# Adding a turned partial result in PSUM: read in its order of storage, written through a view by columns

## The chip, the core and the metric

The kernel runs on one core of a Trainium2 chip. The metric is device time in microseconds (us) of one execution, the median over several runs. Lower is better.

## The reference

Two layers of a vision state-space model are applied in a row to x of 8 images, 64 by 64 positions, 192 channels. Each layer is `x = x + conv(gn(x))`: group normalisation, an input projection to 384 channels and a gate z, a depthwise 3 by 3 convolution with SiLU, a selective scan over the 4096 positions, layer normalisation over channels, multiplication with the activated gate, and an output projection.

The selective scan runs in several directions. In layer 0 there are two: by rows, forward and backward. In layer 1 there are four: by rows and by columns, each forward and backward. For each direction, every channel and each of 16 states:

```
h = exp(delta * A) * h + (delta * u) * B        # along the positions
y = sum over the 16 states of h * C
```

The y of all directions are summed at each position (a direction by columns has to be turned back to rows first), and the skip term `u * D` is added.

## The kernel before, in words

Each layer runs a `front` (normalisation, projections, convolution) and then `scans`. The change is in `scans`.

The positions of an image are cut into 8 chunks of T = 512, and the 384 channels into DT = 3 tiles of 128 partitions. A *step* i is one chunk of one direction of one image. Layer 0 has 8 x 2 x 8 = 128 steps, layer 1 has 8 x 4 x 8 = 256. Layer 1's directions are, in order: columns forward, columns backward, rows backward, rows forward. A step has NSL = 24 *slots*, one for each pair of states (8) and each channel tile (3). Within a slot:

- `inject` (L763, matmuls L773) lets TensorE write (delta * u) * B for two states into a PSUM tile `hb`. It runs two slots ahead, and `hb` has two buffers. Its moving operand takes two neighbouring floats out of every eight (L776).
- `decay` (L783, L790) lets ScalarE compute the factors `da`, four slots ahead.
- `scan` (L801) lets VectorE run two scans along the positions (L817), and after every third slot lets POOL multiply h by C (L820) into `hc`.
- `reduce` (L827) lets TensorE sum `hc` over the states into the PSUM tile `py` (3 banks of 512 floats).

`reduce` and `add_y` both use `block_diag` (L172, matmuls L176): four matmuls on 32 by 32 pieces of the array for each channel tile, so 12 for three tiles. TensorE's fp32 matmul shows as two records.

At the end of a step `keep_y` (L874) copies `py` to SBUF and `store_y` (L884) stores it to the DRAM tensor `yrow` or `ycol`. Before that, `add_y` (L868) adds into `py` what is already there to be summed: the input times the skip weights in the first direction, or an earlier direction's sum through `mask` (an identity in 32 by 32 pieces).

Layer 1's third direction is the first by rows after two by columns. It has to take the sum of the column directions, which lies in `ycol` by columns, and bring it into `py`, which lies by rows. `load_turned` (L851) issues DMAs in slots 8 to 19 which bring, for the chunk's RB = 8 image rows, 64 columns of 8 floats each into the tile `yt`: in SBUF the 8 floats of one image column lie together. The view `live[i]["y"]` (L856) reads this tile by rows, so that neighbouring elements of the view are 8 floats apart. `add_y` then runs in slot 27, which is three slots into the next step, and `keep_y` in slot 29.

The order of all instructions is written out by hand. `at(i, s, f, ...)` enters a function for slot s of step i, tables such as `L1_SLOTS` (L108) give the slots, and the loop at L1099 to L1111 issues `scan`, then the entries of the slot in order of rank, then `inject` for two slots later and `decay` for four slots later. The finishing work of the previous image (`f_...`: normalisation, gate, output projection) is entered in the same way.

The lines around the turned sum:

```
live[i]["yt"] = s1.tile([P, DT, T], F32, name="y")                            # L855
live[i]["y"] = live[i]["yt"].rearrange("p t (w h) -> p t h w", h=RB)          # L856
...
block_diag(nc, live[i]["py"], w, live[i]["y"][:, dt], dt, False, False)       # L872
...
at(i, slots["add_turned"], add_y, i)                                          # L1048
```

Of the kernel before, what the change touches and what calls it, by code (L numbers as in the profile page):

```python
# [18 lines left out]
W = 64  # L19
# [9 lines left out]
RB = T // W  # L29
# [18 lines left out]


L0_SLOTS = {  # L50
    "turn_b": 1,
    "keep_b": 2,
    "dt_proj": (6, 3, 4),
# [52 lines left out]
    "f_add": (111, 113),  # L106
}
L1_SLOTS = {  # L108
    "x_proj": (1, 1, 3),
    "x_dbl": 4,  # L110
    "turn_b": 7,
# [60 lines left out]
def block_diag(nc, out, w, x, dt, first, last):  # L172

    for i in range(NQ):
        j = (i + dt) % NQ
        nc.tensor.matmul(  # L176
            out[j * Q : (j + 1) * Q, dt],
            w[i * Q : (i + 1) * Q],
            x[i * Q : (i + 1) * Q],
            start=first,  # L180
            stop=last,
            tile_position=(i * Q, j * Q),
        )
# [372 lines left out]
def scans(tc, name, x_src, x_dst, xcd, xcd_col, xtd, xdd, zd, t, dirs, rank, row_b, gate, slots, last, ends, consts, dram):  # L556
# [5 lines left out]
    nc = tc.nc  # L562
# [8 lines left out]
    def tiles(a):  # L571
        return a.rearrange("(t p) l -> p t l", p=P)
# [17 lines left out]
    with tc.tile_pool(name=f"{name}_s1", bufs=1) as s1, tc.tile_pool(  # L590
# [7 lines left out]
        def at(i, s, f, *a):  # L598
            todo.setdefault(i * NSL + s, []).append((f, a))

        live = {}
# [249 lines left out]
        def load_turned(i, j):  # L851

            b, k, cols, rev, ci, c = steps[i]
            if j == 0:
                live[i]["yt"] = s1.tile([P, DT, T], F32, name="y")  # L855
                live[i]["y"] = live[i]["yt"].rearrange("p t (w h) -> p t h w", h=RB)  # L856
            dt, q = divmod(j, 4)
            cs = slice(q * W // 4, (q + 1) * W // 4)
            yt = live[i]["yt"].rearrange("p t (w h) -> p t w h", h=RB)[:, dt, cs]
            yd = tiles(ycol[b % 2])[:, dt].rearrange("p (w h) -> p w h", h=H)[  # L860
                :, cs, c * RB : (c + 1) * RB
            ]
            e = dt * Q
            nc.sync.dma_start(out=yt[: P - e], in_=yd[e:])
            if e:
                nc.sync.dma_start(out=yt[P - e :], in_=yd[:e])

        def add_y(i):  # L868
            k = steps[i][1]
            for dt in range(DT):  # L870
                w = t["skip"][:, dt] if k == 0 else mask
                block_diag(nc, live[i]["py"], w, live[i]["y"][:, dt], dt, False, False)  # L872

        def keep_y(i):  # L874
            b, k, cols, rev, ci, c = steps[i]
# [3 lines left out]
        def same(i):  # L879

            b, k, cols = steps[i][:3]
            return k > 0 and dirs[k - 1][0] == cols and b < B - 1
# [131 lines left out]
        def thrice(i, s, f, *a):  # L1014
            for p, q in enumerate(s):
                at(i, q, f, *a, p)

        for i in range(N):
            j = i - 1
            live[i] = {}  # L1020
            at(j, -3, load_xt, i)
            if xdd is None:
                at(j, -8, load_x, i)
                thrice(j, slots["x_proj"], x_proj, i)
                at(j, slots["x_dbl"], x_dbl, i)
            else:
                at(j, -4, load_xdbl, i)
            at(j, slots["turn_b"], turn_b, i)
            at(j, slots["keep_b"], keep_b, i)
            for dt in range(DT):  # L1030
                for f in dt_proj, dt_bias, turn_delta, make_dut:
                    at(j, slots[f.__name__][dt], f, i, dt)
            at(j, slots["softplus"], dt_softplus, i)
            at(j, slots["softplus"] + 1, first_decays, i)
            at(j, 14, enter, i, 0)
            at(j, NSL + 1, enter, i, 1)
            at(i, -12, load_b, i, 0)
            at(i, 0, load_b, i, 1)
            for m in range(NP):
                at(i, 3 * m - 6, load_c, i, m)  # L1040
                at(i, 3 * m + 3, carry, i, m)
                for n in range(2):
                    at(i, 3 * m + slots["reduce"][n], reduce, i, m, n)
            b, k, cols, rev, ci, c = steps[i]
            if k and dirs[k - 1][0] != cols:
                for j in range(4 * DT):
                    at(i, 8 + j, load_turned, i, j)
                at(i, slots["add_turned"], add_y, i)  # L1048
            elif not same(i):
                at(i, 6, load_y, i)  # L1050
                at(i, slots["add_y"], add_y, i)
            at(i, slots["keep_y"], keep_y, i)
            at(i, slots["keep_y"] + 1 * same(i), store_y, i)
# [30 lines left out]
        for c in range(NCH):  # L1084
# [4 lines left out]
            for r, fs in enumerate(  # L1089
                (  # L1090
                    (f_act,),
                    (dt_proj, turn_b, turn_delta, f_turn, f_back, f_out, x_proj),
                    (reduce, add_y),
                    (load_b, load_c, load_turned),
                )
            )
            for f in fs
        }
        with tc.manual_schedule(engines=ENGINES):  # L1099
            g = min(todo)  # L1100
            while todo:
                i, s = divmod(g, NSL)
# [11 lines left out]
def vss_layer(tc, name, x_src, x_dst, w, dirs, rank, row_b, gate, slots, last, ends, consts, dram):  # L1114

    with ExitStack() as ctx:
        xcd, xcd_col, xtd, xdd, zd, *dram = dram
        if any(cols for cols, rev in dirs):
            xdd = None
        else:  # L1120
            xcd_col = None
        t = load_weights(tc, ctx, name, w, len(dirs), rank, row_b + 2 * NS, consts[1])
        clear = dram[-1] if xcd_col is None else ()
        early = gate if gate == AF.Silu else None
        front(tc, name, x_src, xcd, xcd_col, xtd, xdd, zd, w["in_proj"], early, t, clear, consts)
        late = gate if early is None else None
        scans(tc, name, x_src, x_dst, xcd, xcd_col, xtd, xdd, zd, t, dirs, rank, row_b, late, slots, last, ends, consts, dram)
# [3 lines left out]
def two_vss_layers(ctx, tc, x, grp_d, w0, w1, out):  # L1131
# [27 lines left out]
    dram = (xcd, xcd_col, xtd, xdd, zd, yrow, ycol, cscr, dgd)  # L1159
    vss_layer(tc, "l0", x, mid, w0, L0_DIRS, 12, 32, AF.Gelu, L0_SLOTS, L0_LAST, L0_ENDS, consts, dram)  # L1160
    vss_layer(tc, "l1", mid, out, w1, L1_DIRS, 96, 96, AF.Silu, L1_SLOTS, L1_LAST, L1_ENDS, consts, dram)

# [63 lines left out]
```

## Time and profile before

| | us |
|---|---|
| median of 3 runs | 24904.81 (24903.24 to 24905.65) |
| profiled execution, its own time | 24896.44 |
| its span, first to last instruction | 24894.7 |
| start of layer 1's first and last scan | 9782.8 and 24837.6 |
| granted TensorE clock, mean | 0.994 of full speed |

| engine | what it does most | busy us |
|---|---|---|
| DVE (VectorE) | scans, L817 | 20778.5 |
| POOL (GpSimd) | h times C, L820 | 20742.4 |
| ACT (ScalarE) | decay factors, L790 | 12245.1 |
| PE (TensorE) | `inject`, L773 | 10887.2 |
| PE (TensorE) | `reduce`, L176 `py<-hc,mask` | 6870.0 |
| PE (TensorE) | `add_y` with the mask, L176 `py<-y,mask` | 204.0 |
| PE (TensorE) | `add_y` with the skip weights, L176 `py<-y,skip` | 156.5 |

How to read the lines: a group gives the line of the code, the engine, the operation, output<-input by the tiles' names, the shapes and the count, then busy time and the mean duration of one in ns, then the engine's idle time before them and what ended it. Busy time of TensorE counts the time in which at least one matmul ran; matmuls on different 32 by 32 pieces of the array run side by side, so the mean duration times the count is more than the busy time. PEld is the loading of weights, which overlaps matmuls.

### The profile page before, as it was taken

The page shows a single profiled execution, that of the slowest core. Times are in us where ns is not written, and L with a number is a line of the kernel's source. Part 1 is how long each engine was busy: PE and PEld are TensorE (multiplying, and loading weights), DVE is VectorE, ACT ScalarE, POOL GpSimd, SP SyncE. Part 2 cuts the span into 40 slices and gives each one's busy share as a digit, 9 for nine tenths or more (in the row PEclk, how much of TensorE's full clock was granted, in tenths as well). Part 3 has the DMA queues.
Part 4 walks back from the last instruction along what each step waited for, and adds up shares of the span by engine and source line. Part 5 has one row for each costly group of instructions (what it writes and reads, how often), then busy time and mean ns, then how long its engine had stood idle before and what let it go on. Part 6 is the DMA issues. An engine that isn't in the chain of part 4 may idle for free.

```text
span 24894.7 us, 773793 instructions
## 1 busy us (share of the span) xinstructions
PE 23122.6 (93%) x331456; PEld 13199.4 (53%) x331456; DVE 23113.1 (93%) x22416; ACT 19698.0 (79%) x39311; POOL 21490.1 (86%) x4439
## 2 busy tenths in 40 slices
PE   9989999999999898999999999999999999999998
PEld 3455555555555434555555555555555555555554
DVE  7799999999999877999999999999999999999997
ACT  6678888888888777777777877877877877877877
POOL 0299999999999802999999999999999999999998
PEclk9999999999999999999999999999999999999999
DMA  5566666667666556676676676676676676676675
GB/s 188 174 157 168 163 163 170 162 165 170 161 165 168 159 212 209 161 160 167 168 169 167 165 169 168 165 168 168 166 168 168 167 168 167 167 168 166 175 173 158
DMA packets 3857278, 4208.94 MB, mean 169 GB/s; under 512 B 2136204, under 2 KB 2368420, under 8 KB 3850788
## 3 DMA queue, kind: packets, MB, share of 16 engines
q1 hardware_dynamic: 3775472, 3970.30, 61.6%
q0 software_dynamic: 67200, 132.13, 3.1%
q8 instruction: 2626, 43.02, 0.7%
q10 hardware_dynamic: 11188, 57.00, 0.6%
q14 instruction: 792, 6.49, 0.1%
HBM read 3412.11 MB, written 746.65 MB: 167 GB/s over the span
## 4 chain that ended last, share of the span: by engine, by line
PE 23%; DVE 22%; ACT 8%; issue 5%; POOL 2%; DMA 0%; DVEq 0%; SPq 0%; POOLq 0%; ACTq 0%
DVE h L817 21%; PE hb L773 10%; PE py L176 8%; ACT da L790 4%; PE pd L613 3%; POOL hc L820 2%; PE pt L661 1%; ACT y L877 1%; PE po L997 1%; DVE dut L736 1%; ACT delta L169 1%; ACT da L798 1%; ACT L169 0%; ACT L685 0%; ACT xn_sq L957 0%
## 5 line engine op out<-in xcount | busy, mean ns | idle before, releaser
L820 POOL TENSOR_TENSOR hc<-h,cr 128x3072 f32<-128x3072 f32 x3072 | 20742.4, 6813 | 3292.9 <-DVE h L817 2088.6
L817 DVE TENSOR_TENSOR_SCAN h<-da,hb 128x512 f32<-128x512 f32 x18432 | 20778.5, 1198 | 1122.3 <-PE hb L773 940.6
L790 ACT ACTIVATE da<-delta,a_neg 128x512 f32<-128x512 f32 x18432 | 12245.1, 713 | 1303.1 <-DVE h L817 1286.4
L773 PEld LDWEIGHTS hb<-dg,dut 64*128 64x128 f32 x147456 | 9226.7, 185 | 6945.3 <-issue 5972.6
L773 PE MATMUL hb<-dg,dut 64*128 64x128 f32 x147456 | 10887.2, 286 | 897.4 <-DVE h L817 885.6
L176 PE MATMUL py<-hc,mask 32*32 32x512 f32 x147456 | 6870.0, 601 | 8.3 <-POOL hc L820 7.4
L176 PEld LDWEIGHTS py<-hc,mask 32*32 32x32 f32 x147456 | 1268.5, 103 | 1661.7 <-issue 1173.1
L798 ACT COPY da<-a 128x2 f32<-128x2 f32 x8064 | 1563.0, 194 | 287.5 <-ACT da L790 0.7
L398 DVE SCALAR_TENSOR_TENSOR tp<-pad,cw,tp 128x512 f32<-128x512 f32 x2112 | 1414.7, 746 | 188.9 <-ACT tp L392 168.1
L661 PE MATMUL pt<-xdbl,w_dt 96*128 96x512 f32 (+1 forms) x2304 | 1300.5, 646 | 36.7 <-ACT delta L675 22.7
L825 ACT COPY st<-h 128x6 f32<-128x6 f32 x2688 | 536.8, 200 | 999.7 <-DVE h L817 999.5
L728 PE MATMUL pq<-ident,delta 128*128 128x128 f32 x4608 | 758.8, 287 | 432.3 <-DVE dut L736 298.6
L877 ACT COPY y<-py 128x1536 f32<-128x1536 f32 x384 | 552.7, 1439 | 695.4 <-PE py L176 662.3
L675 ACT ACTIVATE delta<-pt,dtb 128x512 f32<-128x512 f32 x1152 | 790.8, 686 | 353.8 <-PE pt L661 353.4
L736 DVE TENSOR_TENSOR dut<-pq,xt_k 128x512 f32<-128x512 f32 x1152 | 767.4, 666 | 81.0 <-PE pq L728 81.0
L728 PEld LDWEIGHTS pq<-ident,delta 128*128 128x128 f32 x4608 | 484.5, 141 | 637.0 <-DVE dut L736 415.5
L613 PE MATMUL pd<-x_k,w_x 128*128 128x512 f32 x1536 | 797.3, 628 | 8.5 <-ACT xv L437 8.5
L346 PE MATMUL pi<-x,w_x 128*128 128x512 f32 x1536 | 756.1, 614 | 44.4 <-ACT xv L437 22.2
L997 PE MATMUL po<-yc,w_out 128*64 128x256 f32 (+1 forms) x2304 | 586.5, 468 | 13.4 <-ACT delta L675 8.3
L169 ACT ACTIVATE delta<-delta 128x1536 f32<-128x1536 f32 x384 | 570.5, 1486 | 4.3
L987 POOL TENSOR_TENSOR yc<-yc,g 128x512 f32<-128x512 f32 x384 | 497.9, 1314 | 20.7 <-ACT yc L978 16.3
L685 ACT ACT_TABLE_LOAD x384 | 492.7, 1283 | 6.8
(98 smaller groups left out, 9722.0 us busy)
## 6 DMA issues: line engine op xcount, KB each, us to landing
cr<-cscr SPq DMA_DIRECT2D x2048, 512.0 KB, 4.2
dg<-dgd SPq DMA_DIRECT2D x1536, 512.0 KB, 7.8
cr<-xdd SPq DMA_DIRECT2D x1024, 512.0 KB, 6.2
xt_k<-xtd SPq DMA_DIRECT2D x768, 384.0 KB, 7.1
yrow<-y SPq DMA_DIRECT2D x144, 768.0 KB, 6.7
zd<-zo SPq DMA_DIRECT2D x192, 512.0 KB, 3.0
xcd<-xo SPq DMA_DIRECT2D x128, 768.0 KB, 3.5
xtd<-xv SPq DMA_DIRECT2D x128, 768.0 KB, 3.6
```

Of the source, the lines that this page charges most:

```text
L176: nc.tensor.matmul(out[j * Q : (j + 1) * Q, dt], w[i * Q : (i + 1) * Q], x[i * Q : (i + 1) * Q], start=first, stop=last, tile_position=(i ...
L398: nc.vector.scalar_tensor_tensor(tv, window(dt, c, s), cw[:, dt, s : s + 1], tv, ALU.mult, ALU.add)
L613: nc.tensor.matmul(live[i]["pd"][:R], w_x[:, dt, k, :], live[i]["x"][:, dt], start=(dt == 0), stop=(dt == DT - 1),)
L661: nc.tensor.matmul(pt, w_dt[:, k, dt * P : (dt + 1) * P], live[i]["xdbl"][:rank], start=True, stop=True,)
L728: nc.tensor.transpose(pq[:, g], live[i]["delta"][:, dt, g * P : (g + 1) * P], ident)
L736: nc.vector.tensor_mul(live[i]["dut"][:, dt], live[i]["pq", dt], live[i]["xt"][:, :, dt * P : (dt + 1) * P])
L773: nc.tensor.matmul(hv[:, r, q], live[i]["dut"][r * G : (r + 1) * G, dt, q], dg[r * G : (r + 1) * G, q, :, 2 * mm : 2 * mm + 2], start=True ...
L790: nc.scalar.activation(da[:, n].rearrange("p (r g j) -> p r g j", r=2, j=G), live[i]["delta"][:, dt].rearrange("p (g r j) -> p r g j", r=2 ...
L798: nc.scalar.copy(da[:, :, f], live[i]["a0"][:, dt, 2 * m : 2 * m + 2])
L817: nc.vector.tensor_tensor_scan(o, a, v, init, ALU.mult, ALU.add)
L820: nc.gpsimd.tensor_mul(hc, h, cr)
L997: nc.tensor.matmul(o, w_out[:, dt, P:] if u else w_out[:, dt, :P], y, start=(dt == 0), stop=(dt == DT - 1), tile_position=(0, h * G),)
```

## The change

For the turned y, `add_y` reads the tile `yt` in the order in which it lies (64 columns of 8 floats, 512 in a row), and gives the matmul an output view of `py` in the same order: for each image column the 8 rows, which are 64 floats apart in PSUM. The same sums land in the same places. In the other uses of `add_y` nothing changes. The slots of `enter` and `load_b` are now read from the tables, with the values that stood in the code (the old `at(i, -12, ...)` is `at(j, 12, ...)` of the step before, j = i - 1).

```diff
 L0_SLOTS = {
+    "enter": 14,
+    "load_b": 12,
...
 L1_SLOTS = {
+    "enter": 14,
+    "load_b": 12,
...
                 live[i]["yt"] = s1.tile([P, DT, T], F32, name="y")
-                live[i]["y"] = live[i]["yt"].rearrange("p t (w h) -> p t h w", h=RB)
...
         def add_y(i):
             k = steps[i][1]
+            py, y = live[i]["py"], live[i].get("y")
+            if y is None:
+                y = live[i]["yt"].rearrange("p t (w h) -> p t w h", h=RB)
+                py = py.rearrange("p t (h w) -> p t w h", w=W)
             for dt in range(DT):
                 w = t["skip"][:, dt] if k == 0 else mask
-                block_diag(nc, live[i]["py"], w, live[i]["y"][:, dt], dt, False, False)
+                block_diag(nc, py, w, y[:, dt], dt, False, False)
...
-            at(j, 14, enter, i, 0)
+            at(j, slots["enter"], enter, i, 0)
...
-            at(i, -12, load_b, i, 0)
+            at(j, slots["load_b"], load_b, i, 0)
```

## The prediction, made before the changed kernel ran

> **What bounds the kernel now.** I read the page first. Four engines are busy for most of the span, so the shares name no bound.
>
> ```profile
> PE 23122.6 (93%) x331456; PEld 13199.4 (53%) x331456; DVE 23113.1 (93%) x22416; ACT 19698.0 (79%) x39311; POOL 21490.1 (86%) x4439
> ```
>
> Next I took the groups of instructions that write or read the tile py, because the change touches only those. Columns: engine, operation, count, then shortest, median and longest duration in ns.
>
> ```profile
> L176 PE MATMUL py<-y,skip x3072: 587/587/612, 1141.2 to 23341.1; 32*32 32x512 f32 x192
> L176 PE MATMUL py<-y,mask x2112: 587/1074/1097, 8176.1 to 24818.2; 32*32 32x512 f32 x192
> ```
>
> Each fp32 matmul leaves two records. Both rows have the same shape (32 by 32 weights, 512 columns), yet one has a median of 587 ns and the other of 1074. The count explains the second row. One `add_y` is 12 matmuls, so 24 records. `py<-y,mask` has 2112 = 88 x 24: 24 calls on a y loaded as it is used, all in the last image, and 64 calls (8 images by 8 chunks of layer 1's third direction) on the turned y. Counted one by one in the trace, all 64 turned calls have medians near 1084 and the others 587 to 600. The turned call reads single floats 8 floats apart (L856). A step of 32 B by itself is not what costs:
>
> ```profile
> L773 PE MATMUL hb<-dg,dut 64*128 64x128 f32 x147456 | 10887.2, 286 | 897.4 <-DVE h L817 885.6
> ...
> L728 PE MATMUL pq<-ident,delta 128*128 128x128 f32 x4608 | 758.8, 287 | 432.3 <-DVE dut L736 298.6
> ```
>
> `inject` (L773) reads pairs of floats, pair after pair 8 floats apart, and takes 286 ns for 128 columns, as much as the transposes of L728 (287), which read 128 floats in a row. So reading singles 32 B apart nearly doubles a record, reading pairs 32 B apart costs nothing. [...]
>
> Is the long call on the path? I compared TensorE's timeline, then VectorE's, at the place where the turned call runs (four slots into the next chunk's scan), once in layer 1's second direction, which adds no y there, and once in the third. Columns: start and length in us, instructions, idle time before them.
>
> ```profile
> 10301.77 2.12 PE L773 MATMUL hb<-dg,dut 64*128 64x128 f32 x32
> 10303.82 1.12 PE L613 MATMUL pd<-x_k,w_x 128*128 128x512 f32 x2
> 10304.87 1.11 PE L176 MATMUL py<-hc,mask 32*32 32x512 f32 x24
> 10305.92 1.19 PE L773 MATMUL hb<-dg,dut 64*128 64x128 f32 x16
> ```
>
> ```profile
> 10757.91 2.12 PE L773 MATMUL hb<-dg,dut 64*128 64x128 f32 x32
> 10759.96 1.12 PE L613 MATMUL pd<-x_k,w_x 128*128 128x512 f32 x2
> 10761.02 1.11 PE L176 MATMUL py<-hc,mask 32*32 32x512 f32 x24
> 10761.90 2.77 PE L176 MATMUL py<-y,mask 32*32 32x512 f32 x24
> 10764.60 1.19 PE L773 MATMUL hb<-dg,dut 64*128 64x128 f32 x16
> ```
>
> ```profile
> 10759.25 4.55 DVE L817 TENSOR_TENSOR_SCAN h<-da,hb 128x512 f32<-128x512 f32 x4 [1.12 <-PE hb L773]
> 10765.91 4.55 DVE L817 TENSOR_TENSOR_SCAN h<-da,hb 128x512 f32<-128x512 f32 x4 [2.10 <-PE hb L773]
> ```
>
> TensorE has no gap here. The next `inject` begins 4.15 us after the previous one without the turned call (10301.77 to 10305.92) and 6.69 us after it with the call. VectorE then waits 2.10 us for that `inject`; at the same place of the second direction (10303 to 10313) it scans without such a wait. Last, the table of busy time by stretches, over eight chunk bodies without a turned call and the eight of the same image with it (image 0), and the same for image 1:
>
> ```profile
> 10295.20:10751.40 456.20, 418.01 (x6368) 245.99 (x6368) 443.87 (x410) 354.49 (x701) 443.15 (x87) 1.00 0.63 153
> 10751.40:11225.60 474.20, 438.58 (x6560) 252.72 (x6560) 445.44 (x409) 354.42 (x701) 433.09 (x79) 1.00 0.77 165
> 12157.10:12624.50 467.40, 436.17 (x6456) 255.07 (x6453) 447.20 (x414) 371.95 (x754) 451.21 (x95) 1.00 0.65 160
> 12624.50:13105.10 480.60, 453.64 (x6646) 260.30 (x6644) 448.37 (x413) 371.80 (x753) 440.76 (x87) 1.00 0.79 172
> ```
>
> The first number is the length. In image 0 a turned call costs (474.20 - 456.20) / 8 = 2.25 us of time, all of the VectorE wait, and nothing gives it back within the chunk. From image 1 on the previous image's finishing work runs alongside, and the cost is (480.60 - 467.40) / 8 = 1.65 us on average: some of it lies beside other delays. So TensorE sets the time at these 64 places.
>
> **The change, part by part.** (1) The view of y in `load_turned` (L856) goes, and `add_y` now reads y in the order in which it lies. (2) The same 12 matmuls write PSUM through a view by columns: eight floats of one column of the image, each 64 floats from the last. (3) `enter` and `load_b` take their slots from the tables, with the same slots 14 and 12; the second counts 12 past the chunk before instead of 12 ahead of its own, which with 24 slots to a chunk is the same place. The instruction lists of both kernels agree on all five queues, waits included, except for 768 matmuls whose output is now 64 by 8 instead of 512. So part 3 costs nothing, no DMA, wait or queue moves, and the whole change is 64 calls x 12 matmuls with another duration.
>
> The read. It becomes 512 floats in a row; such records are the 587 of `py<-y,skip`. How much shorter does the call get? Layer 0 has the same sequence (a `reduce`, an `add_y` with the mask, an `inject`) with y read in a row, in the last image:
>
> ```profile
> 8175.25 1.11 PE L176 MATMUL py<-hc,mask 32*32 32x512 f32 x24
> 8176.13 1.33 PE L176 MATMUL py<-y,mask 32*32 32x512 f32 x24
> 8177.40 1.20 PE L773 MATMUL hb<-dg,dut 64*128 64x128 f32 x16
> ```
>
> From the start of the `reduce` to the start of the `inject` it takes 8177.40 - 8175.25 = 2.15 us, against 10764.60 - 10761.02 = 3.58. The read alone therefore gives 1.43 us per call. The wait of 2.10 is longer than that, so in image 0 all of it shortens the wait: 0.67 stays. Some chunk bodies from image 1 on are already held up by finishing work. The average extra of 1.65 leaves room for 1.43, but counting bodies one by one, those at two of eight positions show about 1.1 against the first direction's. So: 48 x 1.43 + 16 x 1.1 = 86, and 64 x 1.43 = 92 if those bodies give all. I take 90 us.
>
> The write. No TensorE instruction of the trace writes PSUM with gaps: L773, L613, L661, L728 and L176 all write runs. It is bounded from below by nothing extra, the 587 of a run (a gain beyond it is excluded, since no row of this shape is faster), and from above by the nearest row with gaps, the strided read: 1074. At 1074 the call is as long as before and the change is worth nothing. I take the lower end. An fp32 record handles a column in (587 - 286) / (512 - 128) = 0.78 ns, so the write has that long for one float; no row here shows that PSUM needs more, and the row of pairs shows that gaps alone need not cost.
>
> [...]
>
> Sum: the profiled execution took 24896.44 us (span 24894.7); less 90 is 24806. The median of the runs shown is 24904.81, 8.4 above it, so 24815 us there, 0.36% faster.
>
> **Rivals.** *The write costs what the read did.* Single floats with gaps between them hold TensorE up when written as they do when read; records stay between 685 and 1460 ns. For it: the read's own row shows what single floats can cost, and the write is made of single floats. Against: the row shows it for reading from SBUF alone. At 1074: 24905, no change; at 830, half way, 45 us faster. [...]
>
> *Slower: accumulation pays twice.* These matmuls add to what stands in PSUM, so each float needs a read and a write of its place; if each costs the excess 1074 - 587 = 487, the record takes 587 + 2 x 487 = 1561. A call has two rounds of records, so it grows by 2 x 0.487 = 0.97 us over today's, on a TensorE without a gap there: 64 x 0.97 = 62 us, 24967. It decides from where records pass 1460 ns (0.2% is 50 us, 0.78 us per call, 0.39 per record over 1074). Against: `reduce` accumulates in runs at 601 ns mean, so adding is hidden there.
>
> *The gain is swallowed.* Another engine keeps the chunk bodies long. POOL is the candidate: 443 of 456 us in the first stretch. Against: bodies without the call run at 57.0 us in image 0 with more POOL work, and those with it would only come from 59.3 to 57.9. If only the two-of-eight limit held everywhere, 64 x 1.1 = 70 us, 24835: still faster.
>
> *The change does not do what it says.* If the instructions still walked y by singles, records stay 1074. The instruction list shows the 64 by 8 output, so I give this no chance of its own.
>
> **How the numbers follow.** Forecast (gain 70 to 96, the last from 3.58 less two blocks of 1.04 us, times 64): 0.62. The write eats the read's gain, in part or wholly: 0.21, of which 0.02 is still faster by over 0.2%. Slower: 0.14. Swallowed down to 70: 0.03, still faster. About 0.2%, 50 us, is what a measurement of this kernel can tell from no change. So faster 0.67, same 0.19, slower 0.14. The range: 24905 - 96 = 24809, with 9 us for the scatter between the profiled and the other runs, 24800; above, the write's upper end, 24905, with the same scatter 24912. It leaves out the slower rival, 0.14. The forecast's own range is 24800 to 24840.
>
> **What would show it.** Right: the turned records near 590 to 610 ns instead of 1074; `reduce` to `inject` at those 64 places near 2.15 us instead of 3.58; VectorE's wait behind them near 0.7 instead of 2.10; the eight bodies of image 0 near 462.8 instead of 474.2; all else as before. Wrong: records that stay above 685 (the write costs), or short records with the bodies still at 474 (the gain is swallowed; look at what VectorE then waits for).

## The result, and the profile after

The changed kernel takes 24852.15 us (median of 12 runs, 24841.71 to 24864.51) where the kernel before takes 24905.23 (12 runs beside it). The ratio is 0.9978, with a 95% interval of 0.9971 to 0.9986: 53 us less, where 90 were forecast. The profiled execution took 24851.96 us, its span is 24850.2.

First the groups that write or read `py`, by operation (count, then shortest, median and longest in ns). L176 of the kernel before is L180 now, L773 is L777, L817 is L821.

```profile
L180 PE MATMUL py<-hc,mask x147456: 584/612/1059, 1116.8 to 24807.1; 32*32 32x512 f32 x200
...
L180 PE MATMUL py<-y,mask x2112: 584/587/613, 8181.1 to 24772.7; 32*32 32x512 f32 x192
```

The turned call's records went from 1084 ns to 587. The view of PSUM by columns does not show in them: the median of the group is now 587 (1074 before), and its longest record 613 (1097).

Next TensorE's and VectorE's timelines around one turned call of image 0, the third (start, length, instructions, idle time before them).

```profile
10883.49 2.12 PE L777 MATMUL hb<-dg,dut 64*128 64x128 f32 x32
10885.54 1.13 PE L617 MATMUL pd<-x_k,w_x 128*128 128x512 f32 x2
10886.59 1.11 PE L180 MATMUL py<-hc,mask 32*32 32x512 f32 x24
10887.48 1.81 PE L180 MATMUL py<-y,mask 32*32 32x512 f32 x24
10889.22 1.19 PE L777 MATMUL hb<-dg,dut 64*128 64x128 f32 x16
```

```profile
10884.83 4.55 DVE L821 TENSOR_TENSOR_SCAN h<-da,hb 128x512 f32<-128x512 f32 x4 [1.12 <-PE hb L777]
10890.53 7.89 DVE L821 TENSOR_TENSOR_SCAN h<-da,hb 128x512 f32<-128x512 f32 x7 [1.15 <-PE hb L777]
```

From the start of `reduce` (10886.59) to the start of `inject` (10889.22) it is 2.63 us, also the median of the 64 calls. It was 3.58, and 2.15 were forecast. VectorE waits 1.15 us behind it: 2.10 before, 0.67 forecast. So the records are as short as forecast, but the call of 24 records is not: it takes 1.81 us where layer 0's call with the same records took 1.33. That is half a microsecond a call which the prediction had put down to the read.

The table by stretches (length, then busy time of PE, PEld, DVE, ACT, POOL; clock, DMA share, GB/s), for the same chunk bodies as before: image 0 without and with the turned call, then image 1.

```profile
10303.80:10760.00 456.20, 417.99 (x6368) 245.99 (x6368) 443.86 (x410) 354.46 (x701) 443.12 (x87) 1.00 0.64 152
10760.00:11228.30 468.30, 431.98 (x6560) 252.90 (x6560) 445.50 (x410) 354.72 (x701) 432.92 (x79) 1.00 0.78 167
12158.60:12625.30 466.70, 435.46 (x6456) 254.17 (x6453) 447.13 (x414) 371.80 (x754) 451.11 (x95) 1.00 0.66 160
12625.30:13098.80 473.50, 446.16 (x6646) 260.39 (x6644) 448.30 (x412) 371.84 (x753) 440.61 (x87) 1.00 0.81 174
```

Bodies without the call are as long as they were (456.20 in image 0). Those with it went from 474.20 to 468.30 and from 480.60 to 473.50. Over all eight images they take 3787.0 us, against 3838.4 before (both summed in the traces): 51 us less, about the whole change. The medians differ by 53 us, the two profiled executions as wholes by 44.

### The profile page after: what moved, and what is told of

It is laid out like the page before. It is cut to its first block, busy times and chain, and to the rows that moved or that the text cites. A ratio compares the mean times of both kernels' runs of the same rounds, so it can differ in the third digit from the quotient of the medians.

```text
span 24850.2 us, 773793 instructions
## 1 busy us (share of the span) xinstructions
PE 23071.3 (93%) x331456; PEld 13201.6 (53%) x331456; DVE 23112.0 (93%) x22416; ACT 19695.4 (79%) x39311; POOL 21483.6 (86%) x4439
## 4 chain that ended last, share of the span: by engine, by line
PE 23%; DVE 22%; ACT 8%; issue 5%; POOL 2%; DMA 1%; SPq 0%; DVEq 0%; POOLq 0%; ACTq 0%
DVE h L821 21%; PE hb L777 10%; PE py L180 7%; ACT da L794 4%; PE pd L617 3%; POOL hc L824 2%; PE pt L665 1%; ACT y L884 1%; PE po L1004 1%; DVE dut L740 1%; ACT delta L173 1%; ACT da L802 0%; ACT L173 0%; ACT L689 0%; ACT xn_sq L964 0%
## 5 line engine op out<-in xcount | busy, mean ns | idle before, releaser
L821 DVE TENSOR_TENSOR_SCAN h<-da,hb 128x512 f32<-128x512 f32 x18432 | 20777.5, 1198 | 1078.5 <-PE hb L777 901.8
L777 PEld LDWEIGHTS hb<-dg,dut 64*128 64x128 f32 x147456 | 9227.6, 185 | 6894.0 <-issue 5913.7
L777 PE MATMUL hb<-dg,dut 64*128 64x128 f32 x147456 | 10888.8, 286 | 903.0 <-DVE h L821 887.3
L180 PE MATMUL py<-hc,mask 32*32 32x512 f32 x147456 | 6874.2, 601 | 11.1 <-POOL hc L824 8.7
L180 PEld LDWEIGHTS py<-hc,mask 32*32 32x32 f32 x147456 | 1269.2, 103 | 1665.3 <-issue 1183.5
```

Of the source, the lines that this page charges most:

```text
L180: nc.tensor.matmul(out[j * Q : (j + 1) * Q, dt], w[i * Q : (i + 1) * Q], x[i * Q : (i + 1) * Q], start=first, stop=last, tile_position=(i ...
L777: nc.tensor.matmul(hv[:, r, q], live[i]["dut"][r * G : (r + 1) * G, dt, q], dg[r * G : (r + 1) * G, q, :, 2 * mm : 2 * mm + 2], start=True ...
L821: nc.vector.tensor_tensor_scan(o, a, v, init, ALU.mult, ALU.add)
```

## What the instruction list says, and two theories

The waits of the call stand in the built program's list: first layer 0's call in the last image, then the first turned call.

```
py<-y,mask 32x512  [DMAHW0]                                 py<-y,mask 32x64x8  [DMAHW2,DMAHW1,DMAHW0]
py<-y,mask 32x512 x3                                        py<-y,mask 32x64x8 x3
py<-y,mask 32x512  [DMAHW1]                                 py<-y,mask 32x64x8  [DMAHW4,DMAHW5,DMAHW2,DMAHW0]
py<-y,mask 32x512 x2                                        py<-y,mask 32x64x8 x2
py<-y,mask 32x512  [DMAHW2]                                 py<-y,mask 32x64x8  [DMAHW6,DMAHW3,DMAHW1]
py<-y,mask 32x512  [DMAHW3]                                 py<-y,mask 32x64x8  [DMAHW4,DMAHW7,DMAHW2,DMAHW0]
py<-y,mask 32x512                                           py<-y,mask 32x64x8
py<-y,mask 32x512  [DMAHW4]                                 py<-y,mask 32x64x8  [DMAHW3,DMAHW5,DMAHW1,DMAHW0]
py<-y,mask 32x512                                           py<-y,mask 32x64x8
```

In both, five of the twelve matmuls wait. Layer 0's wait for one semaphore each, 5 in all; the turned ones for three or four, 18 in all, because 20 DMAs bring the turned y. **Theory W**: the checks of 13 more semaphores cost the 0.48 us, although the data have landed. **Rival P**: the write by columns costs it between the records.

There is a third possibility, **rival L**: some of the data land late. A run on ready data cannot tell it from W, since it takes away both, but the traces can. These are 19 of the 24 weight loads (PEld) of one call: the turned call of before, layer 0's call of before, and the turned call of the changed kernel.

```profile
10761.90 0.90 PEld L176 LDWEIGHTS py<-y,mask 32*32 32x32 f32 x19 [0.30 <-issue]
8176.14 0.42 PEld L176 LDWEIGHTS py<-y,mask 32*32 32x32 f32 x19 [0.30 <-issue]
10887.48 0.90 PEld L180 LDWEIGHTS py<-y,mask 32*32 32x32 f32 x19 [0.30 <-issue]
```

They take 0.90 us in both turned calls and 0.42 in layer 0's: the 0.48 us stands here, before the change too. In the trace one semaphore is waited for by the weight load itself (each of the 18898 weight loads that wait has one); the others stand before it as entries of their own in TensorE's queue (EVENT_SEMAPHORE, for one or two semaphores). From such an entry to the next step that waits it takes 0.11 us in the median of the 64 calls' 484 entries, and 0.07 to 0.14 in 96% of them. Layer 0's call has no such entry. Of the 64 turned calls, 50 have 8 (for 17 or 18 semaphores) and take 2.63 us from `reduce` to `inject` in the median; 14 have 6 (for 16 semaphores) and take 2.42. The kernel before has 3.58 and 3.37. The length goes by the number of entries, and 34 of the 50 calls lie within 0.02 us of each other; late data would give lengths that vary, as they do in slot 23 below, where TensorE waits 6.16 us in the call shown. So L falls as the cause of the 0.48 us, and it is the entries that cost, not each semaphore.

## Experiments: waits or write

**Ready data.**

```diff
             if y is None:
-                y = live[i]["yt"].rearrange("p t (w h) -> p t w h", h=RB)
+                y = w_x.rearrange("p t k r -> p t (k r)").rearrange("p t (w h) -> p t w h", h=RB)
                 py = py.rearrange("p t (h w) -> p t w h", w=W)
```

> The changed kernel, but the turned call reads layer 1's projection weights, which have lain in SBUF since the start, in place of the column directions' sum (which is left out of the result); the view of PSUM by columns and the 20 DMAs stay. Measured of the changed kernel: turned records of 587 ns, yet reduce to inject at the turned call takes 2.63 us and not the 2.15 of layer 0's call, and its time is 24852. Theory W: the other 0.48 us is the waits, since the turned call's matmuls wait for 17 or 18 DMA semaphores and layer 0's for 5. Then reduce to inject is 2.15 here and the time 24852 - 64 x 0.48 = 24821. Rival P: the view by columns costs the 0.48 between the records. Then 2.63 and 24852 stay.

TensorE's timeline of that run:

```profile
10774.47 1.11 PE L180 MATMUL py<-hc,mask 32*32 32x512 f32 x24
10775.35 1.33 PE L180 MATMUL py<-w_x,mask 32*32 32x512 f32 x24
10776.62 1.19 PE L777 MATMUL hb<-dg,dut 64*128 64x128 f32 x16
```

The call takes 1.33 us, `reduce` to `inject` 2.15 (all 64 lie between 2.14 and 2.15), and VectorE's wait behind it is 0.66. The eight bodies of image 0 take 462.50 us, where the prediction had named 462.8. The view by columns is still there. The time is 24831.1 us (median of 6, ratio 0.9969, interval 0.9958 to 0.9981): 21 us below the changed kernel where 31 were expected, with runs from 24814 to 24847; the length of the call decides, the time alone would not. P falls; W holds, since the traces have ruled out L.

**Write in a run.** The other side of the same question.

```diff
             if y is None:
-                y = live[i]["yt"].rearrange("p t (w h) -> p t w h", h=RB)
-                py = py.rearrange("p t (h w) -> p t w h", w=W)
+                y = live[i]["yt"]
```

> The changed kernel, but the turned call writes PSUM in a run, without the view by columns, so that its sum lands at the wrong positions (the turn is left out); the loads and waits stay. Theory W (the waits cost 0.48 us a call): reduce to inject stays 2.63 us, time 24852. Rival P (the view costs it): 2.15 us and 24821.

The median of `reduce` to `inject` stays 2.63 us, and the time is 24849.03 (ratio 0.9976, interval 0.9967 to 0.9986), that of the changed kernel. The view costs nothing.

**The old read of ready data.**

```diff
-                y = live[i]["yt"].rearrange("p t (w h) -> p t w h", h=RB)
-                py = py.rearrange("p t (h w) -> p t w h", w=W)
+                y = w_x.rearrange("p t k r -> p t (k r)").rearrange("p t (w h) -> p t h w", h=RB)
```

> The read of the kernel before (single floats 8 apart, PSUM written in a run), but of layer 1's projection weights, which have lain in SBUF since the start, in place of the column directions' sum (left out of the result). Theory W: waits and read add up in the kernel before, so reduce to inject falls from 3.58 to about 3.10 us, and the time from 24905 to 24874. Rival: in the kernel before the waits lie beside the long records and cost nothing there; then 3.58 and 24905 stay, and the change itself has brought the waits to light.

```profile
10774.20 1.11 PE L180 MATMUL py<-hc,mask 32*32 32x512 f32 x24
10775.08 2.29 PE L180 MATMUL py<-w_x,mask 32*32 32x512 f32 x24
10777.30 1.20 PE L777 MATMUL hb<-dg,dut 64*128 64x128 f32 x16
```

From 10774.20 to 10777.30 it is 3.10 us, the expected value. The time is 24887.93 (ratio 0.9991, interval 0.9981 to 1.0), where 24874 was expected; the interval touches no change, so here too the call's length decides. So the two costs add up: 3.58 = 2.15 + 0.95 for reading singles + 0.48 for the waits.

**Every sum by columns.** Is the write free only because it is rare?

```diff
-                block_diag(nc, live[i]["py"], mask, hc[:, dt, n], dt, first, last)
+                block_diag(nc, by_col(live[i]["py"]), mask, hc[:, dt, n].rearrange("p (w h) -> p w h", h=RB), dt, first, last)
...
+        def by_col(py):
+            return py.rearrange("p t (h w) -> p t w h", w=W)
```

> The changed kernel, but reduce too writes PSUM through the view by columns, all 147456 records of it, so that the sums over the states land at permuted positions (left as they are). If a write by columns costs nothing for these matmuls: records of 601 ns mean and 24852, as in the changed kernel. If it costs a little that the 1536 turned records hide (a tenth of a record, 60 ns): 6144 reduce calls with two rounds each get longer by 0.12 us, up to 700 us in all, less where TensorE waits anyway. If it costs what reading single floats did: 1074 ns a record, thousands of us.

The group of `reduce` in this run (busy us, mean ns of one):

```profile
L180 PE MATMUL py<-hc,mask 32*32 32x512 f32 x147456 | 6875.3, 601 | 12.4 <-POOL hc L824 10.7 <-issue 1.1
```

In the kernel before it was 6870.0 us and 601 ns, in the changed kernel 6874.2 and 601. The time is 24849.11 (ratio 0.9977, interval 0.9967 to 0.9986). For these fp32 matmuls, writing single floats 256 B apart is as fast as writing a run (601 ns mean). No run here shows other shapes or types.

## Experiments: from the theory to a faster kernel

If the waits cost time, fewer DMAs should give it back, with nothing left out of the result.

**Five loads.**

```diff
             dt, q = divmod(j, 4)
-            cs = slice(q * W // 4, (q + 1) * W // 4)
+            if q:
+                return
+            cs = slice(0, W)
```

> The changed kernel with the turned y loaded by 5 DMAs a chunk instead of 20 (a whole channel tile at a time, in slots 8, 12 and 16). The instruction list then has 4 matmuls of the turned call with one semaphore each, as against 5 with three or four. Theory W (0.48 us a call of waits on many semaphores): reduce to inject 2.15 us, image 0's eight bodies 462.5 us as in the run on ready data, time 24852 - 31 = 24821. Rival: the longer DMAs, each of 8192 pieces of 32 B, land late or hold up the other loads of the same queue; then TensorE or POOL waits for a DMA, and the time is 24852 or more.

```profile
10824.94 1.11 PE L180 MATMUL py<-hc,mask 32*32 32x512 f32 x24
10825.83 1.33 PE L180 MATMUL py<-y,mask 32*32 32x512 f32 x24
10827.09 1.20 PE L777 MATMUL hb<-dg,dut 64*128 64x128 f32 x16
```

```profile
10828.40 6.77 DVE L821 TENSOR_TENSOR_SCAN h<-da,hb 128x512 f32<-128x512 f32 x6 [0.66 <-PE hb L777]
```

`reduce` to `inject` is 2.15 us, VectorE's wait 0.66, and the time 24816.87 us (median of 5, ratio 0.9964, interval 0.9951 to 0.9977). This is the lowest time of the study, and it stands where the prediction had put the change alone (24815): read and waits together are worth what the prediction had put down to the read. The four matmuls that wait have one semaphore each, and the trace has no EVENT_SEMAPHORE entry in the call. Image 0's eight bodies missed what was expected, 466.4 us for 462.5: six take 57.8 to 57.9 us, the first 58.7 and the third 60.7, with a stop inside an `inject` of the kind described further down.

**The call in another place.** What is left is the 0.66 us of waiting behind the call and whatever else the call holds up. In slot 27 it stands among the `x_proj` matmuls that run early in the next chunk. Is there room four slots earlier?

```diff
 L1_SLOTS = {
-    "add_turned": 27,
+    "add_turned": 23,
```

This edit was made to the changed kernel, to the version with five loads, and to the kernel before.

> The changed kernel with the turned call four slots earlier, in slot 23 instead of 27, ahead of the three x_proj matmuls of slots 1, 1 and 3. Theory S: the place sets the price of the call; VectorE waits for no inject in slots 20 to 24 of the bodies without a call, so TensorE has room there, and the bodies fall from 58.3 us to the 57.0 of those without a call: 64 x 1.26 = 81 us at most, 24771. Rival D: the last loads are issued in slot 19 and held up in their queue; then TensorE waits for a DMA at the call, and the gain is gone or turned round.

> Both edits: 5 DMAs, the last in slot 16, and the call in slot 23. Theory S with theory W: bodies of 57.0 us, time 24771, and no wait for a DMA, since the last load has seven slots (15 us) to land. Rival D: if the long DMAs hold up the queue, TensorE still waits for them; 24821 or more.

> The kernel before with the turned call in slot 23. It tells whether the change is worth its 0.95 us a call only in the place where TensorE has no gap. Theory S: the old call of 2.7 us finds room for a part there; some 1.3 us of it as in the changed kernel's run, so 24905 - 81 = 24824, or more if there is more room. If room were no matter, 24905 stays. Rival D as in the changed kernel's run: a wait for the last loads, then 24905 or more.

They took 25443.15 us (ratio 1.0216, interval 1.0201 to 1.0231), 24997.34 (1.0036, 1.0023 to 1.0049) and 25437.44 (1.0214, 1.0197 to 1.0231). In the first of them TensorE's timeline shows why:

```profile
10831.81 1.09 PE L180 MATMUL py<-y,mask 32*32 32x512 f32 x16
10839.05 2.15 PE L180 MATMUL py<-y,mask 32*32 32x512 f32 x8 [6.16 <-DMA y<-ycol]
10841.13 1.79 PE L777 MATMUL hb<-dg,dut 64*128 64x128 f32 x16
```

The last third of the call waits 6.16 us for the loads. It is rival D in all three: TensorE's waits for `y<-ycol` at the call add up to 448, 87 and 378 us. The times grow by more than that, by 591, 180 and 532 us over the same kernels with the call in slot 27: in the first run the `inject` behind the wait shown takes 1.79 us and not 1.19, and the granted clock of the three profiled executions is 0.983, 0.991 and 0.984, where it is 0.994 with the call in slot 27. Slot 27 is late enough for the data (in the changed kernel TensorE's weight loads wait 2.0 us for `y<-ycol` in all, its matmuls not at all), and that is what it is good for. The first and the third run also show that the change is worth nothing (25443 against 25437) where TensorE waits for the data anyway.

**Earlier loads and an earlier call**, on top of five loads:

```diff
-                    at(i, 8 + j, load_turned, i, j)
+                    at(i, 7 + 3 * (j // 4), load_turned, i, j)
...
-    "add_turned": 27,
+    "add_turned": 24,
```

The second run has 22 in place of 24.

> 5 DMAs for the turned y, issued in slots 7, 10 and 13 instead of 8, 12 and 16, and the call in slot 24 instead of 27, ahead of the x_proj matmuls. In the run with 5 DMAs the last one was off the queue at 10813 us of its trace, when slot 24 begins; three slots earlier is 6.7 us earlier. Theory S (TensorE has room ahead of x_proj): the bodies go from 57.8 us to nearer 57.0, time 24817 less up to 64 x 0.77 = 49, so 24770 to 24817. Rival D (the data are late, or the loads of C behind them in the queue): TensorE or POOL waits for a DMA, 24817 or more.

> As the run with the call in slot 24, but in slot 22, where no other work of the next chunk is due. Theory S: 24770 to 24800. Rival D, more likely here: the data of the last load are not there yet, TensorE waits, 24900 or more.

In slot 24 it takes 24846.99 us (0.9975, 0.9964 to 0.9985), in slot 22 24830.55 (0.9968, 0.9957 to 0.998). Neither beats five loads in slot 27 (0.9964); the second cannot be told from it. In slot 24 the call's data are there (`reduce` to `inject` 2.14 us in the median, 2.86 at most), but the call now delays the `x_proj` matmuls (ACT's waits for them add up to 380.5 us, against 327.1 with the call in slot 22), and VectorE waits behind those instead. Rival D shows there in another place: in image 2's first body `x_proj` waits 3.74 us for its own load `x_k`, and that body takes 65.4 us. In slot 22 theory S holds for most bodies: at five of eight positions they come down to 57.5 to 58.3 us. But in ten calls, five of them the first of an image's third direction, it takes 2.66 to 7.0 us from `reduce` to `inject` where the others take 2.14: the data are late. A place that has both room and data for all 64 calls was not found.

## Why the prediction was right, and which term was mis-sized

- **TensorE sets the time at the 64 places:** right. Whatever the call lost, VectorE's wait lost: 0.95 of 0.95 us in the changed kernel (2.10 to 1.15), 1.44 in the runs without the many waits (2.10 to 0.66).
- **The read becomes 587 ns a record:** right. **The write costs nothing extra:** right, and shown on 147456 records (601 ns mean with the view and without it); the chance of 0.35 for a write that costs something was the author's estimate from the row of the strided read (1074 ns).
- **"The read alone therefore gives 1.43 us per call":** this step failed. It took layer 0's call as the turned call with a shorter read, but that call also waits for 5 semaphores instead of 18. The read gives 0.95 us; the other 0.48 are the waits, which the change keeps. The trace of before held the hint twice. Its weight loads take 0.90 us in the turned call and 0.42 in layer 0's, as shown above. And the old call of 2.77 us is two rounds of 1.084 plus 0.60, layer 0's call of 1.33 two rounds of 0.587 plus 0.16. What is not in the records, 0.44 us, cannot come from the read.
- **The sum:** with 0.95 in place of 1.43 it is 64 x 0.95 = 61 us instead of 90; 53 were measured and 51 are in the profiled bodies. The typical body gave what the sum says: the median gain over images 1 to 7 is 0.90 to 0.97 us at each of the eight positions. The rest was lost in a dozen bodies with an irregular wait of 0.3 to 1.7 us, mostly some slots behind the call; the trace of before has two such waits. In one of the dozen TensorE stands still in the middle of an `inject`:

```profile
16679.74 0.49 PE L777 MATMUL hb<-dg,dut 64*128 64x128 f32 x2
16681.46 1.19 PE L777 MATMUL hb<-dg,dut 64*128 64x128 f32 x14 [1.23 <-issue]
```

"issue" is time in which the engine waited for nothing that the profile shows. Stops of over 0.5 us within an `inject`, from one matmul's start to the next, occur 5 times in the trace of before, none of them in a body with the turned call; 11 times in that of after, 5 of them in such bodies; and 7 to 10 times in the first four experiments and with five loads. What causes them stays open; no run here tells it apart.

- **No swallowing by another engine:** right. Bodies without the call stayed at 57.0 us in image 0, and those with it did not reach that floor in slot 27.
- **That some bodies would give only 1.1 us:** not put to the test by the changed kernel, whose 0.95 is less. With five loads, the two positions that were doubted gave 1.23 (59.35 to 58.12), the others 1.4: the limit is there, and a little higher than forecast.
- **The range:** the time lies inside the stated one because that reaches up to the write's upper end, which did not occur. The forecast's own range, 24800 to 24840, had a chance of 0.62 and was missed by 12 us. That 53 us are still just over the 50 that the prediction called faster is luck.

## What to carry to other kernels

When a stretch is compared with a like one to price a part of it, compare the waits of the two as well as the shapes, and check whether the difference sits in the records or between them. Here, on a TensorE without a gap, data split over 20 DMAs cost 0.48 us at the first reader although all of it had landed: five of its matmuls waited for three or four semaphores each (2.63 us from `reduce` to `inject`). With 5 DMAs, and one semaphore for each matmul that waits, nothing of it was left (2.15 us). Moving an expensive reader to where its engine has room pays only if the data are there (in slot 23 the time grew by 591 us); look at when the last load leaves its queue first.

## What was not expected of the hardware

- Waits on semaphores that have been reached cost TensorE 0.48 us in twelve matmuls, whether the matmuls' records were 587 ns long (2.63 us from `reduce` to `inject`, 2.15 on ready data) or 1084 (3.58 and 3.10). The cost went by the entries that the queue has beyond one semaphore for each waiting matmul: with 8 of them a call takes 2.63 us, with 6 of them 2.42, with none 2.15; 17 and 18 semaphores in 8 entries take the same.
- TensorE's read of single floats 32 B apart took 1084 ns for 512 columns, against 587 in a row; its read of pairs 32 B apart took 286 ns for 128 columns, against 287 in a row (L773 and L728 of the kernel before); and its write of single floats 256 B apart cost nothing (601 ns mean with and without).
- With five loads, the first part of a channel tile's load took 0.56 us on SP's queue (median of 192), the part that follows it 7.1 us (median of 128), although it is no larger. With 20 loads the medians of the same two lines were 0.60 and 0.70 us.
